# A two-layer perceiver block: five layers in sequence for the whole batch, or as tasks per batch element whose pieces one loop merges

## The chip, the core and the metric

The kernel runs on one core of a Trainium2 chip. The core has a matrix engine (TensorE, "PE" in the profile; its weight loads are the row "PEld"), a vector engine (VectorE, "DVE"), an activation engine (ScalarE, "ACT"), a general engine (GpSimd, "POOL") and a queue that issues the transfers from and to memory (SyncE, "SP"). Each engine works through its own instructions in order; semaphores make one wait for another. The metric is the time of one execution in microseconds (us). The kernel before takes 1223.26 us, the median of three runs between 1222.86 and 1226.22 us.

## The reference

`x` is (2, 256, 256): two batch elements of 256 rows. `ctx` is (2, 4096, 256). Six residual layers follow one another; `LN` is a layer norm without weights.

```python
x = x + xattn0(LN(x), ctx)   # 16 heads of 16, 256 queries on 4096 keys, masked
x = x + attn0(LN(x))         # rmsnorm, input projection, a 4-tap and a 9-tap depthwise convolution
                             # along the rows, small matrices A, Bm, pw, ha, hb, fuse, out
x = x + ffn0(LN(x))          # LN, 8-bit activations x 3-level weights, gelu, LN, the same again
x = x + xattn1(LN(x), ctx)   # one head of 256 on 4096 keys, additive mask
x = x + attn1(LN(x))         # 16 heads of 64, rotary; 8 of the heads causal
x = x + moe(LN(x))           # top 2 of 8 experts, at most 64 rows for an expert, cut in row order over BOTH batch elements
```

In every layer but the last, one batch element needs nothing of the other. In the last, the rows' places at an expert are counted over all 512 rows.

## The kernel before

Rows lie in `self.x` as four tiles of 128 rows (`NT` = 4), two for each batch element. `l0_xattn` (L143) is written with the order of its instructions set by hand: `tile_perceiver` (L1233) runs it under `manual_schedule`, which keeps the program's order on PE, DVE, ACT and POOL. The five other layers are plain functions, called one after another; the framework's scheduler orders their instructions on every engine by its own priorities, and each function closes its pools of on-chip memory when it ends (`es.close()`).

All five do a step for the whole batch: `layernorm` (L102) and `to_T` (L116, transposes on PE with `evac`, L83, copying to on-chip memory by DVE and ACT in turn) for four tiles, projections by `project_T` (L128, matmul L133) on 512 columns. Weights and context pieces of 512 KB go by `load` (L611, DMA L613) to a ring of 24 slots (`open_ring`, L598). The functions:

- `l0_attn` (L622): both convolutions on DVE (`conv`, L680, multiply-add L687), then the small matrices one after another, and `out` at L734.
- `l0_ffn` (L786): `quantize_weight` (L745) and `quantize_act` (L771) on DVE; `first` (L807) up to gelu (L827) for all four tiles, then `second` (L830).
- `l1_xattn` (L863): `scores` (L904) multiplies a tile of 128 queries with 8 blocks of 512 keys (L909), adds the mask on DVE (L912) and takes the maximum over 4096 (L918) before one exponential (L920). `weigh` (L925) transposes the weights (L938) and multiplies them with the context (L930). `interleave` (L972) alternates the blocks of one tile's scores with those of the `weigh` of the tile before.
- `l1_attn` (L978): 16 blocks of projection and rotary (L999 to L1011), values (L1021), then softmax per group of four heads (exponentials L1056, division by the sum on DVE, L1061), and the group before is transposed (L1076) and weighed (L1086).
- `l1_ffn` (L1111): the choice of experts (up to L1163), gathering (L1188), 8 experts (L1209, L1216) and the scatter (L1224). All 16 weight tiles have a slot in the ring from the start.

The last part of the cross attention, `project_out` (L460), ends with the addition at L495; every row of the later layers follows it.

Of the kernel before, what the change touches and what calls it, by code (L numbers as in the profile page):

```python
# [10 lines left out]
F32 = mybir.dt.float32  # L11
# [8 lines left out]
B = 2  # L20
# [7 lines left out]
ROUND = 12582912.0  # L28

# [16 lines left out]
class Kernel:  # L46
# [551 lines left out]
    def open_ring(self):  # L598
        self.ring = self.ctx.enter_context(self.tc.tile_pool(name="ring", bufs=24, side="right"))

    def slot(self, name, shape):
        n = int(np.prod(shape))
        assert n <= 1024
        t = self.ring.tile([P, 1024], F32, name=name, tag="w")[:, :n]
        if len(shape) == 2:
            t = t.rearrange("p (a b) -> p a b", a=shape[0])
        elif len(shape) == 3:
            t = t.rearrange("p (a b c) -> p a b c", a=shape[0], b=shape[1])
        return t

    def load(self, src):  # L611
        t = self.slot("w", src.shape[1:])
        self.nc.sync.dma_start(t, src)  # L613
        return t

    def load_rows(self, src):
        t = self.slot("w", src.shape)
        self.bcast_load(t, src)
        return t


    def l0_attn(self):  # L622
        nc, T, tc = self.nc, self.T, self.tc
        es = ExitStack()
        b1 = es.enter_context(tc.tile_pool(name="b1", bufs=1))
        w_in = [self.load(T["a0_in"][:, k]) for k in range(2)]
        cw = b1.tile([P, 88], F32, name="cw")
        nc.sync.dma_start(cw, T["a0_small"])
        nw, in_b = cw[:, 0:2], cw[:, 2:10]
        dwa_b, sym_b, pw_b, fuse_b = cw[:, 10:14], cw[:, 14:18], cw[:, 18:22], cw[:, 22:26]  # L630
        ha_b, hb_b = cw[:, 26:28], cw[:, 28:30]
        dwa = cw[:, 30:46].rearrange("p (c k) -> p c k", c=4)
        sym = cw[:, 46:82].rearrange("p (c k) -> p c k", c=4)
        aw = b1.tile([P, 4, 16], F32, name="aw")
        nc.sync.dma_start(aw, T["a0_A"])
        bm = b1.tile([16, 512], F32, name="bm")
        nc.sync.dma_start(bm, T["a0_Bm"])
        w_pw = [self.load(T["a0_pw"][:, 2 * k : 2 * k + 2]) for k in range(2)]
        w_ha, w_hb = self.load(T["a0_ha"]), self.load(T["a0_hb"])
        w_fu = [self.load(T["a0_fuse"][:, 2 * k : 2 * k + 2]) for k in range(2)]  # L640
        w_out = self.load(T["a0_out"])
        out_b = b1.tile([P, D], F32, name="out_b")
        self.bcast_load(out_b, T["a0_out_b"])

        self.layernorm(self.xn, self.x)
        h = b1.tile([P, NT, D], F32, name="h")
        mv = self.sm.tile([P, NT, 2], F32, name="mv", tag="mv")
        ms = self.sm.tile([P, NT], F32, name="ms", tag="ms")
        for t in range(NT):
            st = self.sm.tile([P, 6], F32, name="bst", tag="bst")  # L650
            nc.vector.bn_stats(st, self.xn[:, t, :])
            nc.vector.bn_aggr(mv[:, t, :], st)

        nc.vector.tensor_tensor(ms, mv[:, :, 0], mv[:, :, 0], ALU.mult)
        nc.vector.tensor_tensor(ms, ms, mv[:, :, 1], ALU.add)
        rs = self.sm.tile([P, NT], F32, name="rs", tag="rs")
        self.rstd(rs, ms, 1e-6)
        for t in range(NT):
            nc.vector.tensor_scalar(h[:, t, :], self.xn[:, t, :], rs[:, t : t + 1], None, ALU.mult)
        hT = b1.tile([P, 2, NTOK], F32, name="hT")  # L660
        self.to_T(hT, h, scale=nw)

        PAD = 4
        val = b1.tile([P, 4, B, S + 2 * PAD], F32, name="val")
        nc.gpsimd.memset(val[:, :, :, 0:PAD], 0.0)
        nc.gpsimd.memset(val[:, :, :, PAD + S :], 0.0)
        gate = b1.tile([P, 4, NTOK], F32, name="gate")

        def in_out(i, ps):
            if i < 4:  # L670
                nc.scalar.activation(
                    val[:, i, :, PAD : PAD + S], ps.rearrange("p (b s) -> p b s", b=B), AF.Identity,
                    bias=in_b[:, 4 + i : 5 + i],
                )
            else:
                nc.scalar.activation(gate[:, i - 4, :], ps, AF.Sigmoid, bias=in_b[:, i - 4 : i - 3])

        self.project_T(lambda k, i: w_in[k][:, ((i + 4) % 8) * P : ((i + 4) % 8 + 1) * P], 8, hT, 2, in_out)

        def conv(name, taps, n, bias, off):  # L680
            y = b1.tile([P, 4, B, S], F32, name=name)
            for c in range(4):
                nc.vector.tensor_scalar(
                    y[:, c], val[:, c, :, off : off + S], taps[:, c, 0:1], bias[:, c : c + 1], ALU.mult, ALU.add
                )
                for k in range(1, n):
                    nc.vector.scalar_tensor_tensor(  # L687
                        y[:, c], val[:, c, :, off + k : off + k + S], taps[:, c, k : k + 1], y[:, c],
                        ALU.mult, ALU.add,
                    )  # L690
            return y.rearrange("p c b s -> p c (b s)")

        ya = conv("ya", dwa, 4, dwa_b, PAD - 1)
        yb = conv("yb", sym, 9, sym_b, 0)

        ps = self.bank("psA")
        for k in range(4):
            nc.tensor.matmul(ps[:16, :], lhsT=aw[:, k, :], rhs=ya[:, k, :], start=k == 0, stop=k == 3)
        a16 = b1.tile([16, 1, NTOK], F32, name="a16")
        nc.scalar.copy(a16[:, 0, :], ps[:16, :])  # L700
        a2 = b1.tile([P, 4, NTOK], F32, name="a2t")
        self.project_T(lambda k, i: bm[:, i * P : (i + 1) * P], 4, a16, 1, lambda i, ps: self.evac(a2[:, i, :], ps))
        cat = b1.tile([P, 4, NTOK], F32, name="cat")

        def ha_out(i, ps):
            nc.scalar.activation(cat[:, i, :], ps, AF.Identity, bias=ha_b[:, i : i + 1])

        self.project_T(lambda k, i: w_ha[:, k, i * P : (i + 1) * P], 2, a2, 4, ha_out)

        sg = b1.tile([P, 4, NTOK], F32, name="sg")  # L710
        for c in range(4):
            nc.scalar.activation(sg[:, c, :], yb[:, c, :], AF.Sigmoid)
            nc.vector.tensor_tensor(sg[:, c, :], sg[:, c, :], yb[:, c, :], ALU.mult)
        pw = b1.tile([P, 4, NTOK], F32, name="pw")

        def pw_out(i, ps):
            nc.scalar.activation(pw[:, i, :], ps, AF.Identity, bias=pw_b[:, i : i + 1])

        self.project_T(lambda k, i: w_pw[k // 2][:, k % 2, i * P : (i + 1) * P], 4, sg, 4, pw_out)

        def hb_out(i, ps):
            nc.scalar.activation(cat[:, 2 + i, :], ps, AF.Identity, bias=hb_b[:, i : i + 1])

        self.project_T(lambda k, i: w_hb[:, k, i * P : (i + 1) * P], 2, pw, 4, hb_out)
        y = b1.tile([P, 4, NTOK], F32, name="y")

        def fuse_out(i, ps):
            nc.vector.scalar_tensor_tensor(y[:, i, :], ps, fuse_b[:, i : i + 1], gate[:, i, :], ALU.add, ALU.mult)

        self.project_T(lambda k, i: w_fu[k // 2][:, k % 2, i * P : (i + 1) * P], 4, cat, 4, fuse_out)  # L730
        for t in range(NT):
            ps = self.bank("psO")[:, :D]
            for k in range(4):
                nc.tensor.matmul(  # L734
                    ps, lhsT=y[:, k, t * P : (t + 1) * P], rhs=w_out[:, k, :], start=k == 0, stop=k == 3
                )

            tmp = self.sm.tile([P, D], F32, name="tmp", tag="tmp", bufs=2)
            nc.vector.tensor_tensor(tmp, self.xn[:, t, :], out_b, ALU.add)
            nc.vector.tensor_tensor(tmp, tmp, ps, ALU.add)  # L740
            nc.vector.tensor_tensor(self.x[:, t, :], self.x[:, t, :], tmp, ALU.add)
        es.close()


    def quantize_weight(self, pool, w, n, name):  # L745
# [3 lines left out]
        for i, t in enumerate(w):  # L749
            nc.vector.tensor_reduce(  # L750
                tot[:, i : i + 1], t, AX.X if len(t.shape) == 2 else AX.XY, ALU.add, apply_absolute_value=True
            )
# [5 lines left out]
        mean = pool.tile([P, 1], F32, name=f"mean_{name}")  # L758
# [4 lines left out]
        for i, t in enumerate(w):  # L763
            q = pool.tile([P] + list(t.shape[1:]), BF16, name=f"q_{name}_{i}")
            nc.vector.tensor_scalar(t, t, sc, 1.0, ALU.mult, ALU.min)
            nc.vector.tensor_scalar(t, t, -1.0, ROUND, ALU.max, ALU.add)
            nc.vector.tensor_scalar(q, t, -ROUND, None, ALU.add)
# [18 lines left out]
    def l0_ffn(self):  # L786
# [71 lines left out]
        for t in range(NT):  # L858
            second(t, h2[t])
# [479 lines left out]
```

## Time and profile before

The profiled execution took 1223.28 us; its span from the first to the last instruction is 1221.5 us. The profile page lists for each engine its busy time; the answers on stretches of the span list it for each stretch, with the granted TensorE clock (1.00 is full speed).

| stage | stretch of the span, us | length |
|---|---|---|
| `l0_xattn` | 0 to 652.1 | 652.1 |
| `l0_attn` | 652.1 to 756 | 103.9 |
| `l0_ffn` | 756 to 826 | 70 |
| `l1_xattn` | 826 to 998 | 172 |
| `l1_attn` | 998 to 1152 | 154 |
| `l1_ffn` | 1152 to 1221.5 | 69.5 |

A row of the groups view reads: line, engine, operation, output and inputs, shapes, count, busy time and mean nanoseconds of one, and what the engine waited for ahead of it. A float32 matmul appears as two records, so two records of 592 ns that overlap are one product on 512 columns.

### The profile page before, as it was taken

The numbers are of one execution on the slowest core, as the hardware profiler recorded it, in microseconds if no ns is written. First come the engines' busy times: TensorE is split into PE (matmuls) and PEld (weight loads), VectorE is DVE, ScalarE is ACT, GpSimd is POOL, SyncE is SP. The second block draws the span as 40 slices with busy tenths as digits, with TensorE's granted clock in tenths as the row PEclk, the third lists the DMA queues.
The fourth block names the chain that finished last, engine by engine and source line by source line (L and its number), as shares of the span: only waits on it lengthen the run. The fifth ranks groups of instructions, "written<-read, shape, count | busy, mean of one in ns | idle before, by whom it ended". The sixth has DMA issues, their size and how long they took to land.

```text
span 1221.5 us, 20524 instructions
## 1 busy us (share of the span) xinstructions
PE 1058.0 (87%) x8203; PEld 614.3 (50%) x8204; DVE 678.3 (56%) x1243; ACT 461.0 (38%) x926; POOL 401.2 (33%) x424
## 2 busy tenths in 40 slices
PE   6688899999999899999996595239799889888888
PEld 3354455555566555555553143124466663365666
DVE  3168666666754677777505916974344427557330
ACT  2334466666654456666651210210211212336010
POOL 4114577777763467777760000000000000000000
PEclk9788899999999999999996798558899989979879
DMA  9895044444222211221006623110336440000000
GB/s 320 257 272 176 33 116 113 131 113 117 58 62 70 44 45 46 45 45 36 2 1 226 229 69 99 52 38 27 92 115 194 150 138 0 1 1 1 1 1 18
DMA packets 54446, 108.54 MB, mean 89 GB/s; under 512 B 5568, under 2 KB 27968, under 8 KB 52432
## 3 DMA queue, kind: packets, MB, share of 16 engines
q1 hardware_dynamic: 54352, 107.24, 29.4%
q8 instruction: 64, 1.05, 0.4%
q14 instruction: 30, 0.25, 0.1%
HBM read 87.82 MB, written 19.40 MB: 88 GB/s over the span
## 4 chain that ended last, share of the span: by engine, by line
PE 78%; DVE 13%; issue 3%; ACT 3%; DMA 2%; POOL 1%; SPq 1%; POOLq 0%; ACTq 0%; DVEq 0%
PE av L437 12%; PE st L388 9%; PE sT L421 8%; PE psP L133 7%; PE sT L404 6%; PE psS L909 5%; PE psV L346 4%; PE psK L189 4%; PE av L930 4%; PE ot L1086 2%; DVE yb L687 2%; DVE nm L918 1%; PE psR L999 1%; PE psC L448 1%; PE psI L1209 1%
## 5 line engine op out<-in xcount | busy, mean ns | idle before, releaser
L397 DVE CUSTOM_DVE_ANT_0 junk<-st,madd 128x1024 bf16<-128x1024 f32 x256 | 313.2, 1223 | 113.8 <-PE st L388 112.5
L429 POOL TENSOR_TENSOR p<-p,keep 128x512 int32<-128x512 int32 x256 | 327.7, 1283 | 144.9 <-ACT p L427 138.0
L427 ACT ACTIVATE p<-sT 128x512 f32<-128x512 f32 x512 | 277.9, 595 | 180.7 <-PE sT L421 176.3
L421 PE MATMUL sT<-qz,kst 32*128 32x256 f32 x2048 | 214.2, 326 | 0.0
L388 PE MATMUL st<-kst,qz 32*128 32x512 f32 x1024 | 191.3, 450 | 21.3 <-DVE mx L397 21.3
L100 POOL TENSOR_TENSOR rs<-ve,nhalf 128x4 f32<-128x4 f32 (+1 forms) x12 | 11.1, 928 | 502.1 <-DVE ve L99 502.1
L437 PE MATMUL av<-p,v 128*32 128x256 f32 x2048 | 168.5, 395 | 0.5 <-ACT avs L589 0.5
L421 PEld LDWEIGHTS sT<-qz,kst 32*128 32x128 f32 x2048 | 161.2, 189 | 0.7
L388 PEld LDWEIGHTS st<-kst,qz 32*128 32x128 f32 x1024 | 78.1, 186 | 96.6 <-issue 64.9
L411 PE MATMUL sT<-msh,oneb 3*128 3x512 bf16 x512 | 103.8, 388 | 0.0
L404 PE MATMUL sT<-addT,identb 128*128 128x512 bf16 x256 | 99.9, 390 | 0.0
L189 PE MATMUL psK<-ctx,wkv 128*128 128x512 f32 x128 | 65.0, 639 | 7.2 <-DMA ctx<-in_ctxT 7.2
L176 POOL TENSOR_TENSOR part<-kf,part 128x512 f32<-128x512 f32 x32 | 41.6, 1301 | 84.3 <-DVE part L175 75.6
L404 PEld LDWEIGHTS <-identb 128*128 128x128 bf16 x256 | 25.9, 101 | 84.8 <-issue 84.2
L346 PE MATMUL psV<-wkv,ctx 128*128 128x256 f32 x256 | 64.5, 397 | 0.0
L909 PE MATMUL psS<-w,qk 128*128 128x512 f32 x128 | 62.4, 622 | 0.0
L437 PEld LDWEIGHTS av<-p,v 128*32 128x32 f32 x2048 | 42.3, 108 | 37.5 <-POOL p L429 1.4
L912 DVE SCALAR_TENSOR_TENSOR sc<-psS,sb,w 128x512 f32<-128x512 f32 x32 | 24.0, 751 | 66.3 <-PE psS L909 66.3
L930 PE MATMUL av<-w,pT 128*128 128x256 f32 x256 | 59.8, 380 | 0.0
L346 PEld LDWEIGHTS psV<-wkv,ctx 128*128 128x128 f32 x256 | 47.4, 194 | 17.7 <-issue 11.8
L88 ACT COPY pT<-psT 128x512 f32<-128x512 f32 (+2 forms) x24 | 16.7, 696 | 100.9 <-PE psT L938 92.1
L930 PEld LDWEIGHTS av<-w,pT 128*128 128x128 f32 x256 | 46.7, 191 | 5.2
(258 smaller groups left out, 1289.5 us busy)
## 6 DMA issues: line engine op xcount, KB each, us to landing
ks<-part SPq DMA_DIRECT2D x64, 256.0 KB, 2.9
kst<-ks SPq DMA_DIRECT2D x30, 512.0 KB, 6.6
ctx<-in_ctxT SPq DMA_DIRECT2D x24, 512.0 KB, 5.4
w<-in_ctxT SPq DMA_DIRECT2D x16, 512.0 KB, 7.2
w<-in_ctx SPq DMA_DIRECT2D x16, 512.0 KB, 3.7
w<-in_m_w SPq DMA_DIRECT2D x16, 512.0 KB, 4.2
qz<-qs SPq DMA_DIRECT2D x32, 128.0 KB, 6.5
mi<-in_x_maskT SPq DMA_DIRECT2D x16, 256.0 KB, 3.7
```

The source lines that it names most:

```text
L189: nc.tensor.matmul(ps, lhsT=w[:, 0, k, f * P : (f + 1) * P], rhs=ct[:, k, :], start=k == 0, stop=k == 1)
L346: nc.tensor.matmul(ps[:, i, :], lhsT=ct[:, k, n0 : n0 + P], rhs=w[:, 1, k, :], start=k == 0, stop=k == 1)
L388: nc.tensor.matmul(st[:, h, :], lhsT=qz[r : r + 32, i, qc * P : (qc + 1) * P], rhs=kst[r : r + 32, c * 512 : (c + 1) * 512], start=i == 0, ...
L397: nc.vector.tensor_tensor_reduce(out=junk, in0=st, in1=madd[:, qc, c].rearrange("p h a k -> p h (a k)"), scale=1.0, scalar=-1e38, op0=ALU. ...
L404: nc.tensor.matmul(sts[0], lhsT=self.identb, rhs=addT[:, j].rearrange("p a q -> p (a q)"), start=True, stop=False, skip_group_check=True,)
L411: nc.tensor.matmul(sts[h], lhsT=oneb[r : r + 3, :], rhs=msh[r : r + 3, :].unsqueeze(1).to_broadcast([3, 2, S]), start=h >= NADD, stop=Fals ...
L421: nc.tensor.matmul(sts[h][:, a * S : (a + 1) * S], lhsT=kst[r : r + 32, n0 : n0 + P], rhs=qz[r : r + 32, i, :], start=False, stop=i == 1, ...
L427: nc.scalar.activation(p[:, h].rearrange("p a q -> p (a q)"), sts[h], AF.Exp)
L429: nc.gpsimd.tensor_tensor(p[:, 1].bitcast(I32), p[:, 1].bitcast(I32), keep[:, j], ALU.mult)
L437: nc.tensor.matmul(av[c : c + 32, :], lhsT=vf[:, o : o + 32], rhs=p[:, h, a, :], start=j == 0 and par == 0, stop=j == NJ - 1, tile_positio ...
L909: nc.tensor.matmul(ps, lhsT=qk[:, k, t * P : (t + 1) * P], rhs=ctxT[kb][:, k, :], start=k == 0, stop=k == 1)
L930: nc.tensor.matmul(av, lhsT=pT[:, c, :], rhs=cn[i][:, c, :], start=i + c == 0, stop=i == 7 and c == 3)
```

## The change

`l0_xattn` stays. The five functions go; each layer is now a generator for one batch element (`ffn`: for one tile) that issues a piece of its instructions and yields two numbers: PE time of the piece, and how long until its next piece is worth issuing. `run` keeps all tasks whose predecessors are done, and always takes the piece that can start first by these numbers; equal ones go by `rank`. The order that comes out is kept by the engines: the whole kernel now stands under `manual_schedule`. Transfers are still ordered by the framework.

With it go: a ring of 12 slots instead of 24, 19 tiles of 4 KB and 7 of 2 KB a partition for all activations, 6 single PSUM banks and 2 accumulators, memory that is waited for tile by tile (`reuse_waits="tile"`) and not pool by pool; matmuls on 256 columns; half of the 9-tap convolution as matmuls with diagonal matrices, the 4-tap one folded into `A`, `Bm` with `ha` and `pw` with `hb` multiplied once; the cross attention's mask addition and maximum in one instruction per block, its mask loaded for each batch element; divisions, rotary products and several additions on POOL; absolute sums and the last rounding step on ACT.

```diff
+NW, NA, NH = 12, 19, 7
+    def run(self, tasks):
+        pe, done, live = 0.0, {}, {}
+        tasks = dict(tasks)
+        while tasks or live:
+            for n, (g, after) in list(tasks.items()):
+                if all(a in done for a in after):
+                    live[n] = (g, max([done[a] for a in after], default=0.0))
+                    del tasks[n]
+            order = [n for n in self.rank if n in live]
+            n = min(order, key=lambda n: max(live[n][1], pe))
+            g, ready = live[n]
+            start = max(ready, pe)
+            v = next(g, None)
...
+            work, lat = v
+            if work:
+                pe = start + work
+            else:
+                start = ready
+            live[n] = (g, start + lat)
+    def attn_weights(self):
...
+        for k in range(4):
+            nc.gpsimd.tensor_tensor(ak[:, k], aw, dwa[:, :, k : k + 1].to_broadcast([P, 4, 32]), ALU.mult)
+        dg = [self.slot((8, P)) for _ in range(2)] + [self.slot((2, P))]
+        for n in range(18):
+            d = s["dg"][n // 9, n % 9] = dg[n // 8][:, n % 8, :]
+            nc.gpsimd.tensor_scalar(d, self.ident, sym[:, 2 + n // 9, n % 9 : n % 9 + 1], None, ALU.mult)
+        yield 0, 6
...
+    def attn(self, b):
+        self.norm(xn, x)
+        yield 0, 3.5
+        h = self.act("h", 2, D)
+        self.norm([h[:, 0, :], h[:, 1, :]], xn, 1e-6, square=True)
+        yield 0, 3.5
...
+        for i in range(2):
+            c = 2 + i
+            for k in range(9):
+                nc.tensor.matmul(
+                    psb[:, i, :], lhsT=s["dg"][i, k], rhs=val[:, c, k : k + S], start=k == 0, stop=k == 8
+                )
+            taps = s["sym"][:, i, :]
+            nc.vector.tensor_scalar(yb[:, i, :], val[:, i, 0:S], taps[:, 0:1], sym_b[:, i : i + 1], ALU.mult, ALU.add)
+            for k in range(1, 9):
+                nc.vector.scalar_tensor_tensor(
+                    yb[:, i, :], val[:, i, k : k + S], taps[:, k : k + 1], yb[:, i, :], ALU.mult, ALU.add
+                )
...
+            yield 4.0, 4.0 + 2 * i
+    def ffn_weights(self):
+        w1 = [self.load(T["f0_w1"][:, k]) for k in range(2)]
+        w2 = [self.load(T["f0_w2"][:, 4 * k : 4 * k + 4]) for k in range(2)]
+        yield 0, 8
+        s["q1"], s["m1"] = self.quantize_weight(w1, D * 1024, "w1")
+        yield 1, 7
...
+        s["q2"], s["m2"] = self.quantize_weight(w2, D * 1024, "w2")
+        yield 1, 6
+    def load_keys(self, b, kb):
+        if (b, kb) not in self.cts and kb < 8:
+            cols = slice(kb * 512, (kb + 1) * 512)
+            self.cts[b, kb] = self.load(self.T["ctxT"][b, :, :, cols])
+            self.mks[b, kb] = self.load(self.T["x1_mask"].rearrange("(q p) n -> p q n", p=P)[:, :, cols])
+    def xattn(self, b):
...
+        for kb in range(8):
+            self.load_keys(b, kb + 2)
...
+                nc.vector.tensor_tensor_reduce(
...
+                yield 1.75, 1.75
+    def selfattn(self, b):
...
+            nc.gpsimd.tensor_tensor(ri, raw, cst[:, C_COS : C_COS + S].unsqueeze(1).to_broadcast([P, 2, S]), ALU.mult)
...
+                nc.gpsimd.tensor_tensor(
                     p[:, :, :nk], p[:, :, :nk], rc.unsqueeze(2).to_broadcast([P, 4, nk]), ALU.mult
                 )
...
+                yield 0.9, 0.9
+    def rest(self):
...
+        tasks = {
+            "aw": (aw, []),
+            "a0": (self.attn(0), []),
+            "a1": (self.attn(1), ["a0"]),
+            "fw": (self.ffn_weights(), ["a0", "aw"]),
+            "x0": (begin(self.xattn_weights, self.xattn(0)), ["f00", "f01"]),
+            "s0": (begin(self.self_weights, self.selfattn(0)), ["x0"]),
+            "x1": (self.xattn(1), ["x0", "f10", "f11"]),
+            "r0": (self.route(0, one), ["s0"]),
+            "s1": (self.selfattn(1), ["x1", "s0"]),
+            "r1": (self.route(1, one), ["s1", "r0"]),
+        }
+        for b in range(2):
+            for t in range(2):
+                tasks[f"f{b}{t}"] = (self.ffn(b, t), [f"a{b}", "fw"])
+        self.rank = ["a0", "aw", "f00", "f01", "fw", "a1", "f10", "f11", "r0", "s0", "s1", "r1", "x0", "x1"]
+        self.run(tasks)
+        self.experts()
```

`experts` holds what `l1_ffn` did from the gathering on. In it the first product of the next expert (L1209 before) is issued ahead of the second product of this one (L1216).

## The prediction

> **What bounds the kernel now.** I read the page, then stretches of the span by layer, then the chain of waits, then group rows for prices. The page:
>
> ```profile
> span 1221.5 us, 20524 instructions
> PE 1058.0 (87%) x8203; PEld 614.3 (50%) x8204; DVE 678.3 (56%) x1243; ACT 461.0 (38%) x926; POOL 401.2 (33%) x424
> ```
>
> PE looks nearly full, but that is the first layer. By layer (length; PE, PEld, DVE, ACT, POOL busy; clock; DMA share; GB/s):
>
> ```profile
> 0.00:652.10 652.10, 614.91 (x6480) 344.48 (x6480) 382.84 (x699) 350.48 (x688) 391.04 (x413) 0.96 0.35 98
> 652.10:756.00 103.90, 77.47 (x188) 36.03 (x188) 61.82 (x121) 16.46 (x24) 3.02 (x3) 0.84 0.50 174
> 756.00:826.00 70.00, 19.71 (x92) 10.81 (x94) 58.76 (x149) 10.95 (x13) 5.07 (x6) 0.52 0.17 57
> 826.00:998.00 172.00, 150.19 (x576) 99.35 (x575) 65.34 (x91) 27.02 (x27) 1.01 (x1) 0.93 0.40 126
> 998.00:1152.00 154.00, 137.34 (x568) 80.41 (x568) 93.39 (x135) 49.68 (x159) 0.47 (x1) 0.93 0.00 1
> 1152.00:1221.50 69.50, 58.39 (x300) 43.22 (x300) 16.18 (x53) 6.38 (x15) 0.53 (x1) 0.85 0.02 8
> ```
>
> The change can touch only the last 569.4 us. PE is idle there for 126 us: 50 in the feed-forward layer, where DVE is busy 84%, 26 in the layer ahead of it, 22 and 17 in the two attentions, 11 in the experts. Only this, and work taken away, can be won. The chain shows what stands in the way:
>
> ```profile
> 652.17 4.39 DMA w<-in_a_in
> 656.95 8.43 DMA w<-in_a_fuse
> ...
> 691.07 5.30 DVE yb L687 x8
> 697.02 45.51 PE psP L133 x98
> ...
> 870.01 1.72 PE psS L909 x4
> 872.16 1.73 PE av L930 x8
> 873.89 1.72 PE psS L909 x4
> ...
> 891.96 4.42 DVE nm L918
> ```
>
> At first transfers and the convolution, then PE alone. In the cross attention two products on 512 columns take 1.72 us and four on 256 take 1.73: 0.86 and 0.43 each. Between them 0.43 is left for four transposes, 0.107 each. So columns cost the same in halves; nothing is won or lost by 256 columns.
>
> **What the loop makes of the tasks.** Worked through with its yields and `rank` (I take the order from it and no time), the order is: `a0` with `aw`; `a1` with `fw`, then `f00`, `f01`; `f10`, `f11` in the head and first score blocks of `x0`; the rest of `x0` alone; then `s0` with hardly a hole in its own numbers, so `x1` gets only its `q` in at the end; `x1` with `r0`; `s1` alone; `r1`; `experts`. So the two attentions do not overlap between batch elements; what overlaps is `a1` with `f0`, `f1` with `x0`, `r0` with `x1`.
>
> **The sum, stage by stage.**
> *a0, 57 us.* Two norms of 3.3 (two statistics of 0.43+0.18, 0.17, POOL 1.01, two scalings of about 0.4). POOL is in order: the second norm's power (L100) now stands behind 22 operations on the convolution's constants, which wait for `cw` (issued at 652.64, 4.2 to landing: 657). The trace has no such operation: a 128x128 memset takes 0.204, a quarter of a 128x512 product 0.32; I take 0.3, since it reads and writes (4.4 to 7.0 in all). hT is ready at 667, against 661.5 before. Then PE: `hp` half 3.5, input 16x0.43=6.9, `A` in four column strips 3.3 (L437: four such in 0.64 to 0.82), diagonals 18x0.43=7.8, `hp` rest and bias 5, `hB` 0.9, head 3.5, fuse 6.9, out 3.5; 3 for DVE's second tap chain (9 at about 0.41, then 0.9), 2 of hand-offs: 709. If loads start when single tiles are free (first layer's last read of `v` at 638.9), 2.4 less; bounds 50 to 64.
>
> *From there to x0's first norm, 93 us.* `a1`'s norms and transposes 8.6, its input 6.9: 725. Only 3 of 12 ring slots are free for `fw`'s four tiles (9 are held for `a1`), so the last half of `w2` starts to load when `a1`'s input is through: 4.2 landing, 1.3 for the absolute sum, 0.9 to the mean: 732, with PE and DVE waiting. From then DVE is the bound. `w2` 3.4; convolution of `a1` 2x5.2+3.5; its `y` and `x` 2.8; a token tile 16.1 (two norms 4.5, scaling 0.8, first quantization 1.5, 2x0.75, statistics 1.7, 2x1.25, second quantization 3.1, 0.5), for two 32.2; and `rank` lets `f10`, `f11` push 13 of theirs ahead of `f00`'s end; 5 of waits on gelu, PE and POOL: 70, so 802 (80 to 106). Before, the cross attention started at 826.
>
> *x0, 84.* Head 12, scores 32x0.86=27.5, 2 of `f1`'s products, 3.5 to the first exponentials, 64x0.107+64x0.43=34.4, tail 3.5, hand-offs 1. The 4.42 for the maximum is gone, but PE still waits for the exponentials. Bounds 80 to 90.
>
> *s0, 77.* Norm and transposes 5.2, 2.3 for `x1`'s norm queued between; projections and rotary 8x(4x0.43+0.86)=20.7; values 6.9; softmax and weighing 34 (half of the 68 us from 1068.7 to 1137); out 7.2, last weighing 0.9. The division moves to POOL:
>
> ```profile
> L1061 DVE TENSOR_TENSOR p<-p,rc 128x1024 f32<-128x1024 f32 x12 | 14.7, 1222 | 0.3
> L429 POOL TENSOR_TENSOR p<-p,keep 128x512 int32<-128x512 int32 x256 | 327.7, 1283 | 144.9 <-ACT p L427 138.0 <-DVE mx L397 4.5 <-issue 1.7
> ```
>
> On POOL 1024 elements cost 2.5 us by 1283 ns for half of them, twice DVE's 1.22; PE waits some 6 us for the first group, less than two thirds of that after it, since two groups run ahead; paid for by scores of two heads in different rows at once (0.9 for four). Net nothing; bounds 70 to 84.
>
> *x1, 81.* Its `q` is done; 3.5, 27.5, 3.5, 34.4, 3.5 as above, 1 of hand-offs. But the self-attention's weights hold 8 slots through `x1`, leaving 4, with keys and mask two per block. A block's slots come free at its end, and SP loads the next but one while PE has one block (3.44 us) to do. Landing of a key piece took 3.8 to 10.1 us, median 5.4. Two blocks take 3.44+5.4 and an issue of 0.4: 4.6 each, so 6 blocks lose 7.2, in part filled by `r0`'s 3.4: 81 (73 at no loss).
>
> *s1, 75*: `s0` without `x1`'s norm. *r1 and experts, 66.5*: 14.5 (norm 3.3, 1.9, 1.4, DVE 5, places 2.5), then 52 as from 1169.6 to the end: the chain there has no gap between first and second product for the new order to close. Bounds 62 to 70.
>
> *Costed at nothing.* Mask and maximum in one DVE instruction: by L397 (1223 ns for 1024, 83 to read the maximum) 0.7 a block beside 1.72 of PE; uncovered it would be 11 us an element. Table loads on ACT (1283 ns each, three in these layers): the order keeps sigmoid, gelu, exponential apart, up to four more if not, on an engine 38% busy. The experts' 16 weight tiles: 4 slots are free during `s1`, 6 more after its values, 2 after its output, so SP has 12 loaded when `r1`'s 14.5 us end; uncovered, 4.2 us a tile. `s0`'s weights queue on SP behind the last context pieces of `x0` and ahead of `x1`'s first keys; slots come free through the 34 us of weighing.
>
> Sum: 652.1+57+93+84+77+81+75+66.5=1185.6, against 1221.5: 35.9 less. The profiled run took 1223.28, as good as the median 1223.26, so 1187. The bounds on all stages together give 1137 to 1250.
>
> A DVE operation on two on-chip operands beside POOL shows this in the first layer, and then with POOL idle (min/median/max ns):
>
> ```profile
> L478 DVE SCALAR_TENSOR_TENSOR cxo<-mean,none,cxo x2: 481/994/1508, 420.4 to 422.6; 128x256 f32<-128x256 f32 x2
> L478 DVE SCALAR_TENSOR_TENSOR cxo<-mean,none,cxo x2: 478/482/485, 644.4 to 645.6; 128x256 f32<-128x256 f32 x2
> ```
>
> The Trainium skill ("SBUF — State Buffer", section "Who interferes with whom") says why, and speaks against moving products to POOL: a VectorE instruction with two SBUF inputs and a GpSimd one that reads SBUF block each other for a whole instruction. The 1508 agrees. By the rule each of the 16 rotary additions may wait one POOL product (1.28): DVE then has 0.69+0.69+1.28=2.66 a block against PE's 2.58, so 1 us more in all: 1188 instead of 1187.
>
> **The rivals.** *The pieces merge as the yields say*: DVE does not bind the feed-forward layer; a token tile takes its own chain, about 26 us after `fw` (736), and `x0` starts at 762 instead of 802; the ring costs `x1` nothing: 1187-40-8=1139. For it: three or four chains on one engine hide each other's waits. Against: 65 us of DVE work stand in that stretch by the rows above.
>
> *The ring binds more*: at the worst landing, 10.1 us, two blocks take 13.9: 7 each, +21 instead of 7 over 6 blocks, 14 more; the context pieces of the weighing, one for 4.3 us of PE, lose about 1 each: 1187+22=1209. For it: 12 slots for 24, the mask loaded twice. Against: 126 GB/s were enough before, 308 are seen.
>
> *Kept order costs a wait a piece, slower*: the program's order lets no engine go around a late input. The four token chains have 64 pieces, most ending on another engine. The trace has DVE wait 1.16 for POOL at a norm (5.8 in 5); I counted that. If each piece cost 0.7 more by queueing behind another chain's late one, it is 45: 1232. From 0.63 a piece it is slower. For it: DVE is idle 11 of 70 us even where the scheduler reorders. Against: pieces of other chains stand between.
>
> **How the numbers follow.** Chances: the sum 0.48, merging as planned 0.22, ring 0.10, wait per piece 0.20. The range leaves out half of the second and half of the last: 1139 to 1230. What can be told from no change is 0.3%, 3.7 us: faster is the first three, 0.80; of the last 0.04 lies within, 0.16 is slower.
>
> **What would show it.** DVE near 90% busy from the end of `a0` to `x0`'s norm, at 802; PE waiting on the last `w2` transfer near 725; PE alone without gaps in `x0`, about 84 us; no score blocks of `x1` among `s0`'s; score blocks of `x1` 4.6 apart, 3.44 in `x0`; POOL's division ahead of transposes. Wrong if x0 starts before 780 or after 820, or if the framework keeps slots for `x1` in another way than I read.

## The result, and the profile after

The changed kernel takes 1256.19 us (median of 4 runs, 1254.53 to 1258.73), the kernel before 1223.30 beside it (1222.86 to 1226.22): a ratio of 1.0265, 95% interval 1.0241 to 1.0290. It is 33 us slower; 1187 was predicted. The first layer, whose code is the same, ends at 652.8 us instead of 652.1, so nearly everything happened behind it.

The page of the changed kernel, its first lines:

```profile
span 1255.4 us, 21427 instructions
PE 1077.8 (86%) x8500; PEld 667.5 (53%) x8500; DVE 617.5 (49%) x1264; ACT 480.1 (38%) x991; POOL 484.2 (39%) x521
```

TensorE's busy time grew by 20 us, and VectorE has less to do than before, 617.5 us instead of 678.3. Neither is the loss by itself. The stretches of the changed kernel (start:end and length; busy time of PE, PEld, DVE, ACT, POOL; granted clock; DMA share; GB/s): `a0`; `a1` with `fw` and `f0`; `x0`; `s0`; `x1`; `s1`; `r1` with the experts. They are cut within 1 us of where each task's first norm begins, but `x1` at the end of `s0`, since its norm and first query products stand among `s0`'s.

```profile
652.10:715.50 63.40, 48.39 (x237) 39.76 (x236) 18.50 (x48) 12.12 (x26) 16.45 (x32) 0.87 0.33 112
715.50:813.80 98.30, 52.63 (x230) 39.35 (x230) 60.42 (x156) 23.54 (x39) 12.84 (x26) 0.74 0.21 70
813.80:916.30 102.50, 81.43 (x330) 55.18 (x330) 41.80 (x98) 21.55 (x32) 6.65 (x9) 0.88 0.43 139
916.30:1013.50 97.20, 79.20 (x329) 50.98 (x330) 38.09 (x77) 26.55 (x85) 26.53 (x20) 0.84 0.00 1
1013.50:1100.50 87.00, 73.67 (x298) 50.16 (x296) 29.01 (x90) 14.07 (x25) 2.79 (x3) 0.92 0.48 151
1100.50:1192.70 92.20, 74.65 (x316) 47.95 (x316) 36.20 (x68) 25.97 (x84) 24.28 (x17) 0.89 0.11 37
1192.70:1255.40 62.70, 52.47 (x282) 39.37 (x282) 12.62 (x42) 5.63 (x13) 3.06 (x3) 0.89 0.18 57
```

Against the prediction's sum:

| stage | predicted | measured | off by |
|---|---|---|---|
| `a0` | 57 | 63.4 | +6.4 |
| to `x0`'s norm | 93 | 98.3 | +5.3 |
| `x0` | 84 | 102.5 | +18.5 |
| `s0` | 77 | 97.2 | +20.2 |
| `x1` | 81 | 87.0 | +6.0 |
| `s1` | 75 | 92.2 | +17.2 |
| `r1`, experts | 66.5 | 62.7 | -3.8 |

The order of the tasks was as predicted. In `s0`, where no engine but TensorE has more than 40% to do, TensorE is idle for 18 us and its granted clock is 0.84 on average. What it waited for in the four attentions (engine, tile, releaser: us in total, times, longest):

```profile
PE av L1132 <- DVE pT L1147: 12.0, 2, 6.0
PE ot L1293 <- ACT pT L90: 11.3, 4, 3.6
...
PE ot L1293 <- DVE pT L88: 8.2, 2, 4.1
PE psT L1278 <- POOL p L1263: 7.0, 4, 2.4
PE psT L1144 <- ACT sc L1119: 6.6, 4, 2.5
PE psTb L1014 <- ACT qb L948: 6.3, 1, 6.3
```

The first three, 31.5 us, are waits for *copies* of transposed weights out of PSUM, which take 0.6 to 0.7 us each. The timeline shows why they are late (start, length, engine, line, operation; in brackets the idle time before and what ended it). First `s0`, between the weighing of two groups:

```profile
972.18 0.66 PE L1278 MATMUL psT<-ident,p 128*128 128x128 f32 x4
...
973.77 0.66 PE L1278 MATMUL psT<-ident,p 128*128 128x128 f32 x4
...
974.11 0.18 DVE L1262 RECIPROCAL rc<-su 128x4 f32<-128x4 f32 x1 [1.00 <-ACT p L1258]
...
974.64 0.69 DVE L1254 TENSOR_REDUCE nm<-psS 128x2 f32<-128x512 f32 x1
...
975.45 0.47 ACT L1258 ACTIVATE p<-psS,nm 128x256 f32<-128x256 f32 x1 [1.44 <-DVE nm L1254]
...
976.96 0.47 ACT L1258 ACTIVATE p<-psS,nm 128x256 f32<-128x256 f32 x1
...
977.40 1.07 ACT L90 COPY pT<-psT 128x512 f32<-128x512 f32 x2
...
978.04 1.97 PE L1293 MATMUL ot<-pT,v 128*64 128x256 f32 x4 [3.62 <-ACT pT L90]
```

The transposes are done at 972.8 and 974.4. Their copies stand on ScalarE behind the eight exponentials of the next group, which the program issued first; the last four of them wait for maxima on VectorE (974.64), which stand there behind the reciprocal at 974.11, and that waits for the first four exponentials. TensorE idles 3.62 us and then weighs the next two heads in 1.97 us each, against 1.08 for the two after. In the cross attention it is the sum of the exponentials:

```profile
873.37 1.13 ACT L1119 ACTIVATE sc<-sc,nm 128x1024 f32<-128x1024 f32 x1
873.50 0.16 DVE L1123 TENSOR_REDUCE rc<-su 128x1 f32<-128x4 f32 x1 [7.63 <-ACT sc L1119]
...
874.90 1.27 DVE L1147 COPY pT<-psT 128x512 f32<-128x512 f32 x2
...
875.62 3.78 PE L1132 MATMUL av<-pT,w 128*128 128x256 f32 x8 [6.01 <-DVE pT L1147]
```

VectorE stands 7.63 us at a sum of 0.16 us whose last addend is the seventh of the eight exponentials, and then at the second sum, which needs the eighth; the first copy, which needs two, is behind both.

### The profile page after: what moved, and what is told of

It is laid out like the page before. It is cut to its first block, busy times and chain, and to the rows that moved or that the text cites. A ratio compares the mean times of both kernels' runs of the same rounds, so it can differ in the third digit from the quotient of the medians.

```text
span 1255.4 us, 21427 instructions
## 1 busy us (share of the span) xinstructions
PE 1077.8 (86%) x8500; PEld 667.5 (53%) x8500; DVE 617.5 (49%) x1264; ACT 480.1 (38%) x991; POOL 484.2 (39%) x521
## 4 chain that ended last, share of the span: by engine, by line
PE 77%; DVE 9%; ACT 5%; DMA 3%; POOL 2%; issue 2%; SPq 2%; ACTq 0%; POOLq 0%; DVEq 0%
PE av L439 12%; PE st L390 9%; PE sT L423 8%; PE sT L406 6%; PE av L1132 5%; PE psS L1092 4%; PE psV L348 4%; PE psP L726 4%; PE psK L191 3%; PE ot L1293 3%; PE psP L1188 3%; ACT p L1258 2%; ACT sc L1119 1%; PE psC L450 1%; PE psI L1436 1%
## 5 line engine op out<-in xcount | busy, mean ns | idle before, releaser
L102 POOL TENSOR_TENSOR rs<-ve,nhalf 128x1 f32<-128x1 f32 (+2 forms) x23 | 15.7, 681 | 336.0 <-DVE ve L101 336.0
L1132 PE MATMUL av<-pT,w 128*128 128x256 f32 x256 | 64.6, 399 | 12.0 <-DVE pT L1147 12.0
L1092 PE MATMUL psS<-w,qk 128*128 128x512 f32 x128 | 59.3, 613 | 2.1 <-DMA w<-in_ctxT 1.3
L1132 PEld LDWEIGHTS av<-pT,w 128*128 128x128 f32 x256 | 49.1, 202 | 18.8 <-DVE pT L1147 12.8
L1293 PE MATMUL ot<-pT,v 128*64 128x256 f32 (+1 forms) x128 | 38.7, 436 | 19.4 <-ACT pT L90 11.3
L1263 POOL TENSOR_TENSOR p<-p,rc 128x1024 f32<-128x1024 f32 (+1 forms) x16 | 26.9, 1681 | 69.2 <-DVE rc L1262 61.5
```

Of the source, the lines that this page charges most:

```text
L1092: nc.tensor.matmul(ps, lhsT=qk[:, k, t * P : (t + 1) * P], rhs=ct[:, k, :], start=k == 0, stop=k == 1)
L1132: nc.tensor.matmul(av[:, d, :], lhsT=cn[kc // 4][:, kc % 4, d * P : (d + 1) * P], rhs=pT[:, kk, :], start=kc + d == 0, stop=kc == NKC - 1, ...
```

## Experiments

Theory 1: in-order queues. A copy that TensorE needs stands on VectorE or ScalarE behind work that is not needed yet and waits itself. Rivals: A, the division on GpSimd is what is late; B, weighing head by head is slow by its form. Theory 2 is about the feed-forward and is told below.

How far the times can be compared: the kernel before, run beside each group of these runs, had medians of 1223.3 to 1225.9 us, and the first layer, the same code in all, ended between 651.3 and 656.8 us in the profiles. A difference of less than some 4 us between kernels of different groups is not clear of this; where the profile says more, the time behind the first layer is given too.

**The sum of the cross attention, issued later.**

```diff
         yield 0, 4
-        for t in range(2):
-            rc = self.sm.tile([P, 1], F32, name="rc1", tag="rc1")
-            nc.vector.tensor_reduce(rc, su[:, t, :], AX.X, ALU.add)
-            nc.vector.reciprocal(rc, rc)
-            rcs.append(rc)
...
         add(*before)
+        for t in range(2):
+            rc = self.sm.tile([P, 1], F32, name="rc1", tag="rc1")
+            nc.vector.tensor_reduce(rc, su[:, t, :], AX.X, ALU.add)
+            nc.vector.reciprocal(rc, rc)
+            rcs.append(rc)
         yield 1.75, 2.2
```

> The change, with the sum over the exponentials and its reciprocal of the cross attention issued after the last weighing product, ahead of nothing that TensorE waits for. Theory 1 (VectorE stands at this sum until all eight exponentials are done, with the first copies of transposed weights behind it): the 9.2 us before the first weighing become about 4, so 10 us in two elements, 1246 us. Rival (the first copy waits for its transposes and exponentials anyway, or the weighing then runs into the later exponentials): 1254 to 1258.

1246.60 us (1244.78 to 1247.89), 9.6 less than the change. On the chain only two exponentials are left ahead of the weighing, 2.38 us instead of 9.17, in both elements:

```profile
868.53 2.38 ACT sc L1119 x4
...
1043.93 2.38 ACT sc L1119 x4
```

Shown: the place of these lines cost some 10 us (behind the first layer the profiles differ by 13, 589.3 us for 602.6).

**The division back on VectorE.** The edit is `nc.gpsimd.tensor_tensor` to `nc.vector.tensor_tensor` at L1263.

> The change, with the division of the self-attention's weights back on VectorE. Rival A (GpSimd's 1.9 us, against 1.2, is what the transposes wait for): the 7 us of TensorE's waits for it go, 1247 us or less. Theory 1 (VectorE's queue, with maxima, reciprocals and copies in one order, is what holds the copies up): 16 divisions of 0.7 to 1.2 us more in that queue, so slower by 3 to 15 us, 1259 to 1271.

1274.02 us (1272.91 to 1275.60), 17.8 slower than the change (13.6 behind the first layer), about what was expected or a little more. Rival A falls: the 7.0 us of waits for GpSimd only give way to 8.0 for VectorE's division and the exponentials, and the waits for copies grow from 19.5 to 31.1 us:

```profile
PE ot L1293 <- ACT pT L90: 19.2, 4, 5.3
...
PE ot L1293 <- DVE pT L88: 11.9, 2, 6.0
```

The pieces of the softmax come 4.03 us apart (957.34, 961.37, 965.41) instead of 2.75. So under this order the change's move to GpSimd was a gain of 14 to 18 us. The prediction called it "net nothing".

**The order of the softmax.** First only the pieces moved between the turns:

```diff
-        for hg in [3, 2, 1, 0, None]:
-            if hg is not None:
-                probs[hg] = yield from softmax(hg)
...
+        for hg in [3, 2]:
+            probs[hg] = yield from softmax(hg)
+        for g in [3, 2, 1, 0]:
+            soft = (g - 2, softmax(g - 2)) if g > 1 else None
+            for n in range(4):
+                after = turn(g, probs[g], n // 2, n % 2)
+                if now:
+                    weigh(*now)
+                now = after
+                yield 1.0, 1.0
+                if n % 2 and soft:
+                    yield step()
...
```

> The change, with one thing moved in the self-attention: the two scoring pieces of the group after next are no longer issued ahead of a group's four turns, but one after its second turn and one after its fourth. Theory 1 (queued copies: TensorE waits for copies of transposed weights that stand on ScalarE and VectorE behind the next group's exponentials and maxima, 19.5 us of waits in both elements, and runs at half clock for some 5 us after each): the softmax and weighing fall from 54 us an element to about 42, 24 us in all, 1232 us. Rival A (the wait is that for the division on GpSimd): within 3 us of 1256. Rival B (weighing head by head is slow in itself, by its form and not by its order): 5 us at most, 1251.

1245.98 us (1245.58 to 1253.29), 10 less; in between. Then a fuller rewrite, with three scoring pieces in front, the reciprocal and division behind the next piece's maximum, and the weighing two turns later:

```diff
...
+        for _ in range(3):
+            piece()
+            yield 0.9, 0.9
+        for g in (3, 2, 1, 0):
+            for n in range(4):
+                turned.append(turn(g, probs[g], n // 2, n % 2))
+                if len(turned) > 2:
+                    weigh(*turned.pop(0))
+                yield 1.0, 1.0
+                if n % 2 == 0 and pieces:
+                    piece()
+                    yield 0.9, 0.9
...
```

> The change, with the self-attention's softmax in pieces that stand between the turns: three scoring pieces (a group and a half) ahead of the first turn, then one after every first and third turn; a piece's reciprocal and division are issued after the next piece's maximum; a head is weighed two turns after its own. Theory 1: the three pieces in front come 2.1 us apart instead of 2.75, no copy waits for two pieces' exponentials; 12 us an element less, 1232 us. Rival B (weighing head by head is slow by its form): no better than with the pieces merely moved between the turns, 1244 to 1248.

1249.39 us (1245.89 to 1250.39), no better than the first, close to what rival B gave (1244 to 1248). But the waits were not those of B. The copies of the self-attention cost 1.1 us in both elements, and a new wait had come:

```profile
PE psT L1284 <- POOL p L1238: 19.2, 10, 3.3
```

With a piece less in front the division's 1.9 us had become late. With the late sum added:

> The softmax in pieces between the turns and the late sum of the cross attention together. Theory 1: the gains add, 24 and 10 us, 1222 us, within 0.5% of the kernel before. Rival (they hide one another, or the self-attention's form sets the time): 1234 to 1240.

1233.27 us (1231.10 to 1236.14): of the 34 expected 23 came. Then, on that kernel, `range(4)` for `range(3)`:

> As the run before (softmax in pieces between the turns, late sum), but four scoring pieces ahead of the first turn instead of three. Theory 3 (with three in front the copies no longer wait, and the division on GpSimd has taken their place: TensorE waits 19.2 us for it in the two elements, where the change itself had 7.0): a piece more in front gives each division some 3 us more; of the 19.2 about 6 stay, and the fourth piece costs 2.1 us an element: 9 us less than 1233, 1224 us. Rival B (the form of the weighing): no change, 1231 to 1236.

1215.09 us (1213.75 to 1216.56), 0.9912 of the kernel before (0.9884 to 0.9940): 18 less for one piece in front, twice what was expected. The wait for the division is 5.3 us, 13.9 less, and the clock in `s0` rises to 0.94. The four attentions of this kernel (the first begins 1.2 us behind its cut):

```profile
813.80:910.20 96.40, 81.24 (x332) 54.88 (x330) 42.22 (x98) 21.65 (x32) 6.63 (x9) 0.91 0.44 147
910.20:991.90 81.70, 73.08 (x331) 48.86 (x332) 39.25 (x80) 25.95 (x85) 26.41 (x20) 0.94 0.00 1
991.90:1071.00 79.10, 72.91 (x297) 49.29 (x295) 28.09 (x87) 14.06 (x25) 2.79 (x3) 0.96 0.51 166
1071.00:1149.10 78.10, 70.06 (x316) 46.07 (x316) 36.66 (x72) 25.36 (x84) 24.19 (x17) 0.93 0.13 44
```

Head-by-head weighing is kept here, and each head takes 1.08 us: rival B falls.

Which part carries it? Two runs take back one each from this kernel. One turn instead of two between a head's copy and its weighing (`if len(turned) > 1`):

> The run with four pieces in front (1215 us), but each head is weighed one turn after its own, as in the change, instead of two. If the distance between a copy and its use carries the gain (a copy takes 0.6 to 0.7 us and stands behind up to four exponentials of 0.46 each; one turn is 0.66 and one weighing 1.08): 8 us an element more, about 1231 us. If it is the order of pieces and reciprocals: 1215 to 1219.

1226.59 us (1222.02 to 1228.52), 11.5 more. Reciprocal and division directly behind the exponentials:

> The run with four pieces in front (1215 us), but each piece's reciprocal and division directly behind its exponentials, ahead of the next piece's maxima, as in the change. If the wait of the reciprocal for ScalarE at the head of VectorE's queue carries the gain: pieces 2.75 us apart in front instead of 1.9 (2.5 us an element) and each later copy behind a wait of 1.0 to 1.4 us: 8 us an element more, about 1231 us. If it is only the pace in front: 1220 us.

1219.16 us (1211.77 to 1221.53), 4 more, near the 1220 of "only the pace in front"; the ranges of the two kernels overlap, so by the times alone this is not shown, but the stretches in the last row below are 2.0 and 1.7 us longer. From the first exponential to the output product, on the chain of each kernel (`s0`, `s1`, us; in `s0` the query products of `x1` stand in it):

| kernel | `s0` | `s1` |
|---|---|---|
| the change | 53.2 | 48.6 |
| division on VectorE | 59.1 | 55.6 |
| pieces between turns only | 46.8 | 45.0 |
| three in front, late reciprocal, two turns | 45.2 | 43.2 |
| four in front, late reciprocal, two turns | 36.7 | 34.1 |
| ... one turn | 43.4 | 40.0 |
| ... early reciprocal | 38.7 | 35.8 |

The prediction's 68 us for both elements of the kernel before begin at its first complete run of transposes (1068.7); from its first exponential (1062.0) it took 74.9, 37.4 an element. The prediction's 34 was thus cut some 3 us short, and it was still there to be had, with the same instructions on the same engines, in another order.

**The feed-forward stretch.** The prediction let the last half of `w2` wait for a ring slot. Loaded outside the ring:

```diff
-        w2 = [self.load(T["f0_w2"][:, 4 * k : 4 * k + 4]) for k in range(2)]
+        w2 = [self.load(T["f0_w2"][:, 0:4]), self.act("w2b", 4, D)]
+        self.nc.sync.dma_start(w2[1], T["f0_w2"][:, 4:8])
```

> The change, with the second half of the feed-forward layer's w2 loaded into a tile of the activations' pool, so that it needs no slot of the ring. The prediction's step (the last half of w2 waits for a slot until the second element's input product is through, TensorE and VectorE wait for it): VectorE's wait of 9.0 us at the mean of w2 falls to about 2, 7 us less, 1249 us. Rival (the feed-forward's start waits for the second element's convolution on TensorE anyway): 1253 to 1257.

1261.61 us (1260.13 to 1263.23), 5 slower. The transfer is issued at 701.5 instead of 726.5, and nothing follows from it: the tile's absolute sum starts at 734.84 instead of 734.07, since it stands on ScalarE behind the eight evacuations of `a1`'s input, and VectorE waits the same 9.0 us. The step was wrong: what waits is the queue and not the transfer. The 5 us arise later, in `x1` and `s1` (3 of them in `s1`'s softmax); why was not settled. Then the latencies of the feed-forward's norm and quantization pieces, 1.5 times as long:

```diff
-        yield 0, lat
+        yield 0, 1.5 * (lat)
...
-        yield 0, 2.6
+        yield 0, 1.5 * (2.6)
...
```

> The change, with all the latencies that the feed-forward tasks yield for norms and quantizations taken 1.5 times as long. Theory 2 (the loop, which knows nothing of the engines, takes these steps for faster than they are, since two chains share VectorE; so TensorE stands 4.45 us at the transposes of the quantized tile, the second element's output behind them, and VectorE then 7.32 us at that output): the transposes come later in the order, 6 us less, 1250 us. Rival (another order moves the wait to another place): 1253 to 1260.

1252.85 us (1251.20 to 1253.96), 3.3 less, half of what was expected: the order of the loop costs a little here. The second element's feed-forward behind the first's:

```diff
-                tasks[f"f{b}{t}"] = (self.ffn(b, t), [f"a{b}", "fw"])
+                tasks[f"f{b}{t}"] = (self.ffn(b, t), [f"a{b}", "fw"] + (["f00", "f01"] if b else []))
```

> The change, with the two feed-forward tasks of the second element waiting for those of the first. Theory 2 (the second element's pieces stand on VectorE ahead of the end of the first element's, some 9 us between 787 and 806 of the span, and so ahead of the cross attention's start): it starts 9 us earlier, 1247 us. Rival (the same VectorE work of some 32 us then stands among the masks of the cross attention, whose products wait for it): 1254 to 1260.

1265.18 us (1260.90 to 1265.64), 9 slower (6.8 behind the first layer); theory 2 falls, and the rival's "the same" was too kind. `x0`'s first product comes 4.9 us earlier (814.63), but its exponentials begin at 872.25 instead of 865.44: the pieces now stand in its queues. Behind `x0` altogether (`["x0"]` in place of `["f00", "f01"]`, on the kernel with all gains, below):

> As the run with everything, and the second element's feed-forward waits for the end of the first element's cross attention, so that it stands beside the self-attention's projections and softmax. Theory 2 (these pieces cost some 9 us on VectorE ahead of the cross attention's start and some 8 among its score blocks): 1203 less 17, plus up to 9 of their TensorE time and of queueing in the self-attention: 1190 to 1198 us. Rival (they cost there what they cost elsewhere, since each queue keeps its order): 1201 to 1210.

1213.85 us (1208.95 to 1217.38), 11 slower than that kernel. `x0`'s exponentials start at 840.30 instead of 870.16, 30 us earlier, and all of it and more is lost in `s0`, where TensorE now waits for the feed-forward's tiles and, behind them, for its own (waits between 900 and 1000 us):

```profile
PE psTb L982 <- ACT qa L948: 6.3, 2, 5.5
PE psTb L1014 <- ACT qb L948: 5.9, 2, 5.0
PE psS L1255 <- ACT p L1270: 4.1, 1, 4.1
PE psS L1255 <- DVE v L88: 3.0, 1, 3.0
```

**What else the order left.** The mask into the activations' pool, with keys and mask loaded three blocks ahead instead of two:

```diff
-            self.mks[b, kb] = self.load(self.T["x1_mask"].rearrange("(q p) n -> p q n", p=P)[:, :, cols])
+            self.mks[b, kb] = self.act("mk", 2, 512)
+            self.nc.sync.dma_start(
+                self.mks[b, kb], self.T["x1_mask"].rearrange("(q p) n -> p q n", p=P)[:, :, cols]
+            )
...
-            self.load_keys(b, kb + 2)
+            self.load_keys(b, kb + 3)
...
```

> The softmax in three pieces in front and the late sum, and the mask of the later cross attentions loaded into tiles of the activations' pool instead of the ring's, keys and mask three blocks ahead instead of two. Theory of the prediction's ring step (eight slots of twelve are held by the self-attention's weights, so that keys and mask of the second element come late: 5.0 and 3.9 us on the chain): these waits go, 1225 us instead of 1233. Rival (transfers, not slots, set it; or a mask now waits for a tile that the self-attention holds): 1230 to 1238.

1230.41 us (1227.49 to 1234.62), 3 less than 1233, with ranges that overlap: a gain is not shown. The transfers on the chain hardly held TensorE: it waited 0.9 us for keys without this edit. A named latency at the fourth piece (`yield 0.9, 8.0` for the last of the four):

> As the run with four pieces in front, and the last of these yields a latency of 8 us instead of 0.9, so that the loop puts the second element's query products and its first score block (5.9 us of TensorE in all) into the hole before the first turn, and other score blocks behind the last turns. Theory 4 (the loop left this hole empty because the yields name no latency): 4 us less than that run, about 1220 us if it takes 1224. Rival (the pieces' copies and masks on VectorE and ScalarE stand among the softmax's and hold it up): no less than it.

1210.57 us (1208.10 to 1212.46), 4.5 less than without it, as theory 4 said: the loop fills a hole where the yield names one. The sum of the gains, without and with that latency:

> Four pieces in front, late sum, mask outside the ring three blocks ahead, and the feed-forward's latencies 1.5 times. If the gains add: 1233 less 9, 8 and 3, so 1213 us, faster than the kernel before by 0.9%. Rival (moved waits): 1222 to 1230.

1208.04 us (1202.89 to 1212.60): 5 better than the theory's 1213.

> Everything that gained so far in one kernel: four pieces in front, late sum, a latency of 8 us named at the last of the four, mask outside the ring three blocks ahead, the feed-forward's latencies 1.5 times. If the last step's 4.5 us add to the 1208 of the run without it: 1203 us, 1.8% faster than the kernel before. Rival (the hole is no longer there with the other order of transfers): 1208.

1202.73 us (1198.78 to 1209.66), 0.9815 of the kernel before (0.9785 to 0.9845): faster than the kernel before and than the change. The 5 us between these last two runs lie within their ranges.

## Why the prediction was wrong

*s0, 77, and s1, 75* (measured 97.2 and 92.2; half of the whole error). The failed step is "softmax and weighing 34 (half of the 68 us from 1068.7 to 1137)". The 68 us were those of a kernel whose order a scheduler makes; they were carried over to an order written by hand, where the elements took 53.2 and 48.6 from the first exponential on. Under it copies stand behind the next group's exponentials (19.5 us of waits), and after the long waits the next products run at half speed (the rows are in the last section). "PE waits some 6 us for the first group, less than two thirds of that after it" named the division; that wait was 7.0 us in both elements together. With the order mended the stages took 81.7 and 78.1.

*x0, 84* (102.5). Four terms. "3.5 to the first exponentials" was 10.2 from the first exponential to the first weighing, the sum at the head of VectorE's queue. "2 of `f1`'s products" were 4.0, and a wait of 6.33 us for `f1`'s quantized tile in front of score blocks that were ready was not counted. The first weighing, 3.78 us instead of 1.73 for the same eight, is 2 more; 1.5 us stay open.

*x1, 81* (87.0). The ring step, "4.6 each, so 6 blocks lose 7.2", was too dark: TensorE waited 1.3 us for keys. The time went into the exponentials, as in `x0`; the two errors cancel in part.

*a0, 57* (63.4, inside its bounds of 50 to 64). The terms as written add up to 713, not 709, so 4 us are a slip of addition; without it the whole sum is 1191, still a forecast of "faster". GpSimd's 22 operations, "4.4 to 7.0 in all", took 12.0 us (656.93 to 668.90, the 18 diagonals 0.61 each), some 5 more than allowed. Shorter terms, `A` with 1.93 instead of 3.3 among them, took part of this back.

*From there to x0's first norm, 93* (98.3). The total held; its step on `w2` is refuted above, and "from then DVE is the bound" is wrong, for VectorE is idle a third of that time (busy 61% of the whole stretch, where "near 90%" was the sign), its longest wait 7.32 us, at `a1`'s fuse product, which stood on TensorE behind `f0`'s late transposes.

*r1 and experts, 66.5* (62.7): inside 62 to 70. "Net nothing" for the division left out 14 to 18 us of gain. The 1 us priced for VectorE's rotary additions beside GpSimd did not come: they took 0.89 us by the median instead of 0.69, and VectorE stayed idle 0.9 us in each block.

The third rival, a wait per piece in an order that is kept, ended at 1232 and had a chance of 0.20. Its mechanism is what happened. It was priced over the 64 pieces of the token chains, at 0.7 us each, and not over the attention's turns, where one step of order cost 10 us (the sum) to 18 (a piece in front). What the prediction lacked was a walk through the queues of VectorE and ScalarE in program order, piece by piece; it took TensorE's order from the yields and assumed that the others keep up.

## What to carry to other kernels

When a program's order becomes the engines' order, price every instruction that waits by what stands behind it in its own queue. Issue copies that the bottleneck needs ahead of bulk work for a later group, a sum or reciprocal behind the next piece's start, and leave two steps, not one, between a copy and its use. A duration measured under a scheduler that reorders is no estimate for a hand-written order until its queues are walked. Work that is merged to fill holes is hidden only where no in-order queue carries it ahead of work that is ready: the feed-forward of the second element cost 7 to 11 us more in each of the two other places that were tried.

## What the hardware showed

A wait of TensorE costs more than its length. In `s0` of the change, after waits of 2.04 and 3.62 us in a stretch of little work, two heads in a row were weighed in 1.97 us each and four transposes took 1.12; some 5 us later they took 1.08 and 0.66:

```profile
960.04 1.75 PE L1278 MATMUL psT<-ident,p 128*128 128x128 f32 x7 [2.35 <-POOL p L1263]
...
963.84 1.97 PE L1293 MATMUL ot<-pT,v 128*64 128x256 f32 x4 [2.04 <-ACT pT L90]
...
965.74 1.12 PE L1278 MATMUL psT<-ident,p 128*128 128x128 f32 x4
...
966.78 1.97 PE L1293 MATMUL ot<-pT,v 128*64 128x256 f32 x4
...
968.68 1.04 PE L1278 MATMUL psT<-ident,p 128*128 128x128 f32 x4
...
969.66 1.08 PE L1293 MATMUL ot<-pT,v 128*64 128x256 f32 x4
```

The Trainium skill ("TensorE: Matmul & The Clock Gate", section "Part 1: The HAM clock gate (the 'warmup' mystery)") has the array fall to half of its clock after an idle window of about 3.4 us and come back after as long a busy one. The rows agree on the half and on a few microseconds until it ends. They differ on the length of the wait: 2.04 us was enough here, with 2.35 us of idle time and 1.75 of transposes ahead of it. In the kernel with pieces between the turns single waits of 1.35 and 2.19 us in busier stretches were followed by full speed (1.08 and 0.86). So the length of one wait alone does not decide; where the limit lies was not measured.

What it is worth shows between the kernels with three and with four pieces in front, from the first exponential to the output product (`s0`, `s1` of the first, then of the second):

```profile
950.58:997.22 46.64, 35.66 (x179) 20.88 (x175) 19.34 (x43) 19.66 (x74) 13.40 (x8) 0.89 0.00 1
1120.47:1163.30 42.83, 31.94 (x170) 18.56 (x166) 18.47 (x41) 19.67 (x74) 13.40 (x8) 0.88 0.04 15
...
947.68:984.37 36.69, 32.61 (x178) 19.92 (x174) 19.41 (x43) 19.42 (x74) 13.36 (x8) 0.95 0.00 1
1107.40:1141.51 34.11, 30.02 (x171) 18.00 (x167) 18.54 (x41) 19.42 (x74) 13.35 (x8) 0.95 0.05 18
```

The two stretches are 18.7 us shorter: 13.7 are idle time of TensorE, and 5.0 are busy time for the same products, at a granted clock of 0.95 instead of 0.89 and 0.88.

GpSimd took 1.89 us for the division of 1024 elements, not the estimated 2.5, and 1.04 for 512.
